# Own due times for the first four and the last five graphs of a four-layer graph network

## The chip, the cores and the metric

The kernel runs on one core of a Trainium2 chip. The metric is the device time of one execution in microseconds; before the change it is 2971.6 us, the median of three runs (2968.86 to 2973.91).

## The reference

32 graphs of 512 nodes with 256 features go through four attention layers. All graphs share one adjacency matrix and the weights, and no graph needs another's data. After each layer the result is added to the layer's input and normalised over the features.

```
x = layernorm(x + L0(x))   # 8 heads of 32: softmax(q k^T / sqrt(32), masked) v, layernorm, two matmuls with relu, layernorm
x = layernorm(x + L1(x))   # one head: e = leaky_relu(s1[n] + s2[m]), masked softmax over m, times h = x W
x = layernorm(x + L2(x))   # e = leaky_relu((x W1)(x W2)^T), masked softmax, times x W3, relu
x = layernorm(x + L3(x))   # 4 heads of 64: as layer 1, then elu
```

## The kernel before, in words

All data are float32. A graph's x is four tiles of 128 nodes by 256 features. One graph after the other is described by the same function `graph(b)`, as some 330 steps; each step is one or a few instructions of one engine, with an estimate of its time and the buffers that it reads and writes. Nothing is issued while the steps are described. A planner (`Plan.place`) then walks through the steps of all graphs and fixes the order in which each engine gets them, and each engine's queue runs in that order.

Up to five graphs are in work at once (`WAYS = 5`), so that one graph's matmuls can fill TensorE while another waits for its softmax. The planner takes, among the steps that can start earliest by its estimates, the one with the smallest due time, which `urgency(op)` gives. A step of graph b is due at b times `PACE` (90.30 us) plus a time that depends on where the step stands in the graph: the graph is planned alone once, its span is cut into ten equal parts, and the table `TENTHS` says when each part is due. In the kernel before, all graphs use `TENTHS`, and only the last two have a small offset (`LAST`). `START` holds back the load of x of the first five graphs. `STAY` makes it dearer for TensorE to change between matmuls of different array shapes.

The lines that the text below speaks of, all numbered as in the kernel before, in the order of a graph:

- L1323 loads x, L1330 stores the result (SyncE's queue). L886 transposes x or a normalised y on TensorE, L874 copies a PSUM bank out on ScalarE.
- Layer 0: L899 and L913 project to q, k and v (`wqkv`); L1016 forms scores, L1020 their exponentials (ScalarE), L1068 multiplies p by the adjacency `edge_t` (VectorE), L1075 multiplies by v. L954 adds p tiles by DMA to get the sums of the rows, which L1047 then forms on TensorE; the last graph forms them on TensorE alone (`at_once`). L967, L999 and L1002 bring the result back to nodes and divide; L1112 and L1124 are the two matmuls.
- Layer 1 and layer 3: `gates` makes factors from the scores. L1158 transposes them on TensorE, SyncE writes them to device memory (L1162) and reads them back broadcast over all partitions (L1168). Then VectorE forms p: four L1187 and one L1190 (times the adjacency) in layer 1; four L1266 and one L1273, four times, in layer 3. The products are L1197 in layer 1 and L1282 in layer 3; L1257 forms the sums of layer 3. L1309, L1311 (ScalarE) and L1314 (VectorE) are the elu.
- Layer 2: L899 and L913 again, L1220 forms scores, L1223 to L1229 the softmax, L1236 the product.
- Normalisation: L927 and L928 statistics and L934 a factor on VectorE, L937 on ScalarE. L944 are additions and products on GpSimd.

Of the kernel before, what the change touches and what calls it, by code (L numbers as in the profile page):

```python
# [28 lines left out]

WAYS = 5  # L30
PACE = 90.30
START = (0, 22.9, 53.29, 85.04, 134.37)
LAST = (-0.21, 0.21)
STAY = 4.86
TENTHS = (0, 26.21, 86.69, 92.24, 176.51, 212.02, 277.3, 313.49, 381.31, 382.21, 490.27)
@with_exitstack
def general_path(
    ctx: ExitStack,
# [31 lines left out]
    B, N, C = x.shape  # L70
# [544 lines left out]
def fast_path(  # L615
# [35 lines left out]
    B, N, C = x.shape  # L651
# [45 lines left out]
    plan = Plan({kind: len(tiles) for kind, tiles in buffers.items()})  # L697
# [621 lines left out]
    def graph(b):  # L1319

        at_once = b == B - 1
        xs = Slot("x")
        plan(SP, 450, lambda xs=xs: nc.sync.dma_start(  # L1323
            T(xs), x[b].rearrange("(c p) d -> p c d", p=P)), [], [(xs, c) for c in range(NC)],
            lag=9000)
        for layer in (layer0, layer1, layer2, layer3):
            y = layer(xs, at_once) if layer in (layer0, layer3) else layer(xs)
            xs = Slot("x")
            normalise(y, xs)
        plan(SP, 450, lambda: nc.sync.dma_start(  # L1330
            out[b].rearrange("(c p) d -> p c d", p=P), T(xs)), [xs], [], lag=8000)
# [3 lines left out]

    graph(0)
    alone = plan.place(lambda op: op.rank, 1, run=False)
    due = {}
    for t, op in plan.trace:
        tenth = min(int(10 * t / alone), 9)  # L1340
        due[op.rank] = 1e3 * (TENTHS[tenth] + (TENTHS[tenth + 1] - TENTHS[tenth]) * (10 * t / alone - tenth))
    plan.clear()
    plan.begin(-1)
    prepare()
    for b in range(B):
        plan.begin(b, 1e3 * START[b] if b < len(START) else 0.0)
        graph(b)

    def urgency(op):
        if op.graph < 0:  # L1350
            return op.rank - 1e6 if op.engine is not SP else 1e-3 * op.rank - 1e-3
        return 1e3 * (op.graph * PACE + (LAST[op.graph - B] if op.graph >= B - len(LAST) else 0.0)) + due[op.rank]
    with tc.manual_schedule(engines={mybir.EngineType.PE, mybir.EngineType.DVE,
                                     mybir.EngineType.Activation, mybir.EngineType.Pool,
                                     mybir.EngineType.SP}):
        plan.place(urgency, WAYS, 1e3 * STAY)

# [14 lines left out]
@with_exitstack  # L1372
def kernel(ctx: ExitStack, tc: tile.TileContext, *args):


    flag = ctx.enter_context(tc.tile_pool(name="flag", bufs=1))
    beyond = flag.tile([1, 1], I32, name="beyond")
    with ExitStack() as pools:
        fast_path(pools, tc, beyond, *args)
    with tc.If(tc.nc.values_load(beyond, min_val=0, max_val=1) > 0):  # L1380
        general_path(tc, *args)
# [29 lines left out]
```

## Time and profile before

| | us |
|---|---|
| median of three runs | 2971.6 |
| span of the profiled execution | 2969.2 |
| TensorE busy | 2866.9 |
| VectorE busy | 2293.7 |
| ScalarE busy | 1889.8 |
| GpSimd busy | 958.9 |

A busy share says how much of the span an engine worked; what it lacks to the whole is idle time somewhere. Where it is idle matters more than how much: with five graphs in work the middle of the kernel can be full while the beginning, where the first graphs fill up, and the end, where the last ones run out, are not.

### The profile page before, as it was taken

The page shows a single profiled execution, that of the slowest core. Times are in us where ns is not written, and L with a number is a line of the kernel's source. Part 1 is how long each engine was busy: PE and PEld are TensorE (multiplying, and loading weights), DVE is VectorE, ACT ScalarE, POOL GpSimd, SP SyncE. Part 2 cuts the span into 40 slices and gives each one's busy share as a digit, 9 for nine tenths or more (in the row PEclk, how much of TensorE's full clock was granted, in tenths as well). Part 3 has the DMA queues.
Part 4 walks back from the last instruction along what each step waited for, and adds up shares of the span by engine and source line. Part 5 has one row for each costly group of instructions (what it writes and reads, how often), then busy time and mean ns, then how long its engine had stood idle before and what let it go on. Part 6 is the DMA issues. An engine that isn't in the chain of part 4 may idle for free.

```text
span 2969.2 us, 39737 instructions
## 1 busy us (share of the span) xinstructions
PE 2866.9 (97%) x14262; PEld 1585.3 (53%) x14262; DVE 2293.7 (77%) x4076; ACT 1889.8 (64%) x4104; POOL 958.9 (32%) x898
## 2 busy tenths in 40 slices
PE   8899999999999999999999999999999999999885
PEld 3464555555555555555555555555555555555552
DVE  5567887787877878877877877888887788887775
ACT  5666576665766656766666766666766666676543
POOL 0333233332333323334332233332333333333211
PEclk9999999999999999999999999999999999999988
DMA  7536565565755566665566655566665566662232
GB/s 176 123 77 139 128 146 123 105 146 128 153 125 119 123 139 139 149 132 121 124 149 135 146 124 120 124 151 134 147 137 127 121 135 144 141 149 54 68 73 67
DMA packets 93707, 375.66 MB, mean 127 GB/s; under 512 B 8768, under 2 KB 44736, under 8 KB 57664
## 3 DMA queue, kind: packets, MB, share of 16 engines
q0 software_dynamic: 44640, 292.57, 49.0%
q1 hardware_dynamic: 48864, 80.49, 9.1%
q8 instruction: 114, 1.87, 0.2%
q14 instruction: 89, 0.73, 0.1%
HBM read 63.38 MB, written 17.10 MB: 27 GB/s over the span
## 4 chain that ended last, share of the span: by engine, by line
PE 90%; DVE 4%; DMA 3%; ACT 1%; issue 1%; POOL 0%; SPq 0%; ACTq 0%; DVEq 0%
PE bank L913 15%; PE bank L899 10%; PE bank L1016 8%; PE bank L1075 8%; PE bank L1197 8%; PE bank L1236 8%; PE bank L1282 8%; PE bank L1220 8%; PE bank L886 5%; PE bank L1112 4%; PE bank L1124 3%; PE bank L1047 2%; DMA p<-row 2%; PE bank L999 2%; PE bank L1257 1%; PE bank L967 1%
## 5 line engine op out<-in xcount | busy, mean ns | idle before, releaser
L954 POOL DMA_DIRECT2D p<-p x310 | 273.9, 886 | 1520.4 <-DMA p<-p 522.2
L1020 ACT ACTIVATE p<-bank 128x512 f32<-128x512 f32 x1024 | 546.9, 604 | 156.3 <-PE bank L1016 156.1
L1068 DVE TENSOR_TENSOR p<-p,edge_t 128x2048 f32<-128x2048 f32 x256 | 592.9, 2319 | 56.3 <-ACT p L1020 55.0
L874 ACT ACTIVATE t<-bank 128x512 f32<-128x512 f32 x640 | 369.1, 597 | 343.2 <-PE bank L1282 120.3
L944 POOL TENSOR_TENSOR y<-y,x 128x512 f32<-128x512 f32 x192 | 341.6, 1793 | 283.2 <-ACT y L1311 165.4
L927 DVE BATCH_NORM_STATS2 st<-y 128x6 f32<-128x256 f32 x768 | 314.4, 409 | 21.6 <-POOL y L944 15.3
L1075 PE MATMUL bank<-p,v 128*32 128x512 f32 x2048 | 276.8, 614 | 27.8 <-DVE p L1068 27.0
L1273 DVE TENSOR_TENSOR p<-p,edge_t 128x2048 f32<-128x2048 f32 x128 | 293.1, 2290 | 3.2
L1016 PE MATMUL bank<-t,t 32*128 32x512 f32 x2048 | 295.0, 641 | 0.0
L1266 DVE TENSOR_SCALAR p<-p,e,e 128x512 f32<-128x512 f32 x512 | 252.9, 539 | 31.6 <-DMA p<-row 31.1
L937 ACT ACTIVATE x<-y,rs,rs 128x256 f32<-128x256 f32 x512 | 269.5, 597 | 9.2 <-DVE rs L934 9.2
L1197 PE MATMUL bank<-v,p 128*128 128x257 f32 x1024 | 249.2, 390 | 19.6 <-DVE rs L934 14.8
L1236 PE MATMUL bank<-v,p 128*128 128x257 f32 x1024 | 243.6, 386 | 0.0
L1282 PE MATMUL bank<-p,v 128*64 128x512 f32 x1024 | 242.7, 614 | 0.4 <-DVE p L1273 0.4
L1220 PE MATMUL bank<-t,t 128*128 128x512 f32 x512 | 238.4, 599 | 0.0
L899 PE MATMUL bank<-t,wqkv 128*128 128x512 f32 x512 | 237.8, 597 | 0.0
L874 ACT ACTIVATE v<-bank 128x258 f32<-128x258 f32 (+2 forms) x384 | 172.2, 460 | 96.7 <-PE bank L913 94.1
L1236 PEld LDWEIGHTS bank<-v,p 128*128 128x128 f32 x1024 | 188.0, 190 | 69.6 <-ACT p L1020 21.3
L1197 PEld LDWEIGHTS bank<-v,p 128*128 128x128 f32 x1024 | 192.4, 194 | 59.1 <-issue 34.4
L1016 PEld LDWEIGHTS bank<-t,t 32*128 32x128 f32 x2048 | 82.1, 183 | 167.4 <-issue 112.8
L1241 ACT ACTIVATE y<-bank,rs 128x256 f32<-128x256 f32 x128 | 61.2, 480 | 169.8 <-DVE rs L1239 169.7
L886 PEld LDWEIGHTS bank<-ident,x 128*128 128x128 f32 x1024 | 119.1, 144 | 88.5 <-ACT x L937 36.6
(120 smaller groups left out, 4276.1 us busy)
## 6 DMA issues: line engine op xcount, KB each, us to landing
p<-p POOLq DMA_DIRECT2D x248, 1024.0 KB, 7.5
p<-row SPq DMA_DIRECT2D x32, 1024.0 KB, 6.3
p<-p POOLq DMA_DIRECT2D x62, 512.0 KB, 4.5
x<-in_x_dram SPq DMA_DIRECT2D x32, 512.0 KB, 7.0
out_dram<-x SPq DMA_DIRECT2D x32, 512.0 KB, 2.9
e<-row SPq DMA_DIRECT2D x32, 256.0 KB, 3.1
t<-in_adj_dram SPq DMA_DIRECT2D x4, 256.0 KB, 6.1
wqkv<-in_L_gnn_w_qkv_dram SPq DMA_DIRECT2D x1, 768.0 KB
```

The lines of the kernel that those rows point to most:

```text
L874: act(170 + n * 0.84, lambda: nc.scalar.activation(to(T(dst)), frm(T(src)), AF.Copy), [src], writes)
L899: nc.tensor.matmul(T(bank), T(w)[:, i, col:col + P], T(xT)[:, i, :], start=(i == 0), stop=(i == KC - 1))
L913: nc.tensor.matmul(T(bank)[:, j * width:(j + 1) * width], T(xT)[:, k, (c0 + j) * P:(c0 + j + 1) * P], T(w)[:, k, col:col + width], start=( ...
L944: pool(1500 if row is None else 1850, lambda: nc.gpsimd.tensor_tensor(T(dst)[:, w, :], T(a)[:, w, :], T(b)[:, w, :] if row is None else T( ...
L1016: nc.tensor.matmul(T(banks[j]), T(kT)[r, g, m * P:(m + 1) * P], T(qT)[r, g, :], start=True, stop=True)
L1020: act(600, lambda j=j: nc.scalar.activation(T(p)[:, j, :], T(banks[j]), AF.Exp, scale=1.0 / math.sqrt(D0)), [banks[j]], [(p, j)])
L1068: dve(2420, lambda p=p, m=m: nc.vector.tensor_tensor(T(p), T(p), T(edge_t)[:, m, :].unsqueeze(1).to_broadcast([P, J, N]), ALU.mult), [p, ( ...
L1075: nc.tensor.matmul(T(av)[j * D0:(j + 1) * D0, :], T(v)[:, m, h * D0:(h + 1) * D0], T(p)[:, j, :], start=(m == 0), stop=(m == NC - 1))
L1197: nc.tensor.matmul(T(bank)[:, :C + 1], T(p)[:, m, c * P:(c + 1) * P], T(v)[:, m, 2:C + 3], start=(m == 0), stop=(m == NC - 1))
L1220: nc.tensor.matmul(T(bank), T(xT)[:, k, m * P:(m + 1) * P], T(qT)[:, k, :], start=(k == 0), stop=(k == KC - 1))
L1236: nc.tensor.matmul(T(bank)[:, :C + 1], T(p)[:, m, c * P:(c + 1) * P], T(v)[:, m, :C + 1], start=(m == 0), stop=(m == NC - 1))
L1282: nc.tensor.matmul(T(av)[i * D3:(i + 1) * D3, :], T(q)[:, m0 + m, 2 * H3 + h * D3:2 * H3 + (h + 1) * D3], T(p)[:, 2 * m + i, :], start=(m0 ...
```

## The change

The first four graphs and the last five get tables of due times of their own, each of eleven numbers like `TENTHS`. `LAST` and its two offsets are replaced. Between the two the tables `TENTHS` and the pace stay. The tables of the last five graphs (27 to 31) let the later tenths of graphs 28 and 29 fall due very late (653.82 and 888.75 us after the graph's own start on the scale, where `TENTHS` has 490.27), and those of 30 and 31 earlier in the middle, so that the end of graph 31 comes early among its neighbours and the last three graphs are due together. `START` also changes: graphs 1 to 3 may be loaded at 0, 53.29 and 88.61 instead of 22.9, 53.29 and 85.04. It is a change of order only: every graph keeps its steps. It is meant to fill TensorE where the first graphs start and the last ones end.

```
-START = (0, 22.9, 53.29, 85.04, 134.37)
-LAST = (-0.21, 0.21)
 STAY = 4.86
+START = (0, 0, 53.29, 88.61, 134.37)
+
 TENTHS = (0, 26.21, 86.69, 92.24, 176.51, 212.02, 277.3, 313.49, 381.31, 382.21, 490.27)
+FIRST = (
+    (-14.58, 58.82, -25.93, -24.45, 99.53, 212.02, 277.3, 225.46, 380.43, 381.33, 489.39),
+    (20.46, 79.82, -4.21, 95.49, 168.52, 212.02, 277.3, 315.61, 382.59, 384.58, 492.64),
+    (10.74, 90.74, 6.57, 60.81, 176.51, 212.02, 277.3, 313.49, 383.92, 382.21, 492.29),
+    (-115.77, 26.21, 86.69, 92.58, 176.51, 210.06, 277.3, 313.49, 381.31, 382.21, 487.12),)
+LAST = (
+    (0, 25.88, 86.52, 92.24, 176.3, 211.81, 277.09, 313.28, 381.68, 376.38, 536.57),
+    (0, 27.77, 86.69, 92.22, 176.49, 212, 277.93, 316.39, 400.99, 521.01, 653.82),
+    (0, 26.21, 87.61, 91.24, 177.97, 214.48, 309.58, 343.79, 765.5, 770.4, 888.75),
+    (-0.65, 26.94, 85.87, 100.46, 141.72, 174.63, 259.04, 341.35, 397.71, 410.07, 514.93),
+    (3.71, 25.72, 94.73, 50.65, 70.79, 101.96, 247.58, 292.79, 344.82, 346.48, 489.36),)
...
-    due = {}
-    for t, op in plan.trace:
-        tenth = min(int(10 * t / alone), 9)
-        due[op.rank] = 1e3 * (TENTHS[tenth] + (TENTHS[tenth + 1] - TENTHS[tenth]) * (10 * t / alone - tenth))
+    when = {op.rank: 10 * t / alone for t, op in plan.trace}
+
+    def due(b, rank):
+        times = FIRST[b] if b < len(FIRST) else LAST[b - B] if b >= B - len(LAST) else TENTHS
+        tenth = min(int(when[rank]), 9)
+        return PACE * b + times[tenth] + (times[tenth + 1] - times[tenth]) * (when[rank] - tenth)
...
-        return 1e3 * (op.graph * PACE + (LAST[op.graph - B] if op.graph >= B - len(LAST) else 0.0)) + due[op.rank]
+        return 1e3 * due(op.graph, op.rank)
```

## The prediction

> **What bounds the kernel now.** I read the page's first part for the engine that sets the pace, then the table of stretches for where that engine is not busy, then TensorE's list of waits for the last stretch, then TensorE's timeline there.
>
> ```profile
> PE 2866.9 (97%) x14262; PEld 1585.3 (53%) x14262; DVE 2293.7 (77%) x4076; ACT 1889.8 (64%) x4104; POOL 958.9 (32%) x898
> ...
> PEclk9999999999999999999999999999999999999988
> ```
>
> TensorE is busy 97% of 2969.2 us. Only 102.3 us are idle, so no reordering can bring more than that plus what a lowered clock costs. In the table of stretches (start:end, length, then busy us of each engine, TensorE's clock, DMA share, GB/s) the idle time lies at the two ends:
>
> ```profile
> 0.00:620.00 620.00, 587.44 (x2946) 317.06 (x2947) 452.15 (x794) 387.07 (x831) 180.88 (x184) 0.99 0.60 130
> 620.00:2640.00 2020.00, 2006.10 (x10066) 1114.44 (x10064) 1608.01 (x2838) 1337.49 (x2912) 709.07 (x640) 1.00 0.62 133
> 2640.00:2970.00 330.00, 273.39 (x1257) 153.83 (x1253) 233.51 (x446) 165.22 (x362) 68.97 (x74) 0.91 0.34 79
> ```
>
> The head loses 32.6 us, the middle 13.9 us in 2020, the last 330 us lose 56.6 us, at a clock of 0.91. The waits of TensorE in that last stretch:
>
> ```profile
> PE bank L886 <- ACT x L937: 12.8, 4, 4.8
> PE bank L1257 <- DVE p L1273: 12.0, 1, 12.0
> PE bank L1197 <- DVE rs L934: 11.0, 1, 11.0
> ```
>
> These are dependences inside one graph: transposes of a layer's input waiting for its normalisation, and layers 1 and 3 waiting for the gates to come back through memory and for VectorE to build p. TensorE's timeline (start, us, then the instructions, and in brackets the idle time ahead) shows that the wait is paid twice:
>
> ```profile
> 2786.85 3.77 PE L1197 MATMUL bank<-v,p 128*128 128x257 f32 x8 [11.01 <-DVE rs L934]
> ...
> 2793.62 1.90 PE L1197 MATMUL bank<-v,p 128*128 128x257 f32 x8
> ...
> 2873.34 2.38 PE L886 MATMUL bank<-ident,x 128*128 128x128 f32 x8 [4.47 <-ACT x L937]
> 2876.40 6.35 PE L899 MATMUL bank<-t,l2m 128*128 128x512 f32 x8 [0.69 <-ACT t L874]
> ...
> 2912.69 2.38 PE L886 MATMUL bank<-ident,x 128*128 128x128 f32 x8 [4.77 <-ACT x L937]
> ...
> 2934.18 3.63 PE L1257 MATMUL bank<-p,pick 128*32 128x512 f32 x8 [11.95 <-DVE p L1273]
> ```
>
> The same eight L1197 take 3.77 us after an idle 11.01 us, and 1.90 us in the run of work.
>
> [...]while GpSimd ran three L944 from 2771.03 to 2775.04, one L1187 took 3.08 us; such instructions take 0.52 us elsewhere in VectorE's timeline.
>
> **What the change moves.** No instruction is added or removed in a graph; only urgency() differs, so each engine's queue has the same work in another order. I compared the two orders. TensorE's is identical from its 404th to its 1976th planned step (of 2391), which is from graph 4, layer 2, to graph 26, layer 1, and covers the middle. So the middle costs nothing either way: its 13.9 us of idle stay. What is left is the head (graphs 0 to 5) and the tail.
>
> Head. Graph 0's x is now loaded ahead of wqkv, and TensorE's second step becomes a projection that needs wqkv. x can come a little before the 7.63 us at which TensorE starts today, wqkv some half a microsecond later (one issue on SyncE). I take 0, between -1 and +2 us. Then the order is nearly the same up to the first transposes of graph 0's layer 1; the waits before it stay. After it, the gates' transpose of graph 0 (L1158) and the product that needs them (L1197) had about 6 us of other matmuls between them, and have 16 now (three L899 pairs of graph 4 and several steps of graph 2, by their durations in the timeline). The wait there is 3.82 us, and the L1197 behind it took 3.44 us where 1.75 is normal. That is 3.8 + 1.7 = 5.5 us gained. For graph 1 the same filler shrinks from 21 to 13 us, still above the 10 us that this round trip needs at least. (SyncE's two issues, 3.1 us landing, four L1187 and an L1190 of 2.3 us: L1158 at 2836.21 gives 2846.3 at the earliest.) Some of the gain can be lost at VectorE, so I take -4, between -7 and +2.
>
> Tail, stretch A: from graph 28's layer-3 transposes (2708.3) to graph 31's (2912.7). It lasts 204.4 us. The waits in it are 11.01 + 0.35 + 0.74 + 3.42 + 0.16 + 0.21 + 4.47 + 0.69 + 4.77 = 25.8 us; the slow instructions behind them add 1.87 + 0.87 + 1.87 + 0.55 + 1.34 + 2.65 = 9.2 us (each against the same instruction at full clock). So 169.4 us are matmuls. In the new order four layer-3 products of graph 30 (4 x 1.87), and graph 29's sums, transposes and output transposes (0.9 + 0.4 + 0.9) now stand behind graph 31's transposes: 9.7 us less, 159.7 us left. What happens to the waits:
> - Normalisation to transpose, graph 31's layer 2 (4.47 us) and layer 3 (4.77): today nothing stands between. Now three L1236 steps of graph 30 (5.5 us) and three L1282 of graph 29 (5.6 us) do. From the last matmul to the transpose takes 4.6 and 4.8 us in the timeline, so both are just covered.
> - Gates of graph 31, layer 1: 13 us of filler in place of 11. But VectorE's four L1187 and L1190 now follow each other, where before normalisations stood between them. The round trip needs 10, so 3.4 us can go.
> - Gates of graph 30, layer 1 (11.01 us): 18 us of filler in place of 11, and no run of GpSimd adds beside it.
> Is VectorE fast enough? Its work in the rest of the kernel from 2708.3 is 179.2 us. 52 of them come behind graph 31's transposes now (below), so 127 fall into stretch A, 75 to 80% of it. The middle runs at 1608/2020 = 80% with almost no wait. It fits, but with covers that are only a microsecond longer than what they hide. I allow 10 us for waits that stay or appear (between 2 and 28), most likely where TensorE's in-order queue holds a layer-3 product of graph 28 or 29 that waits for its L1273 on VectorE, with graph 31's projections behind it. Stretch A: 169.7 us, that is -34.7.
>
> Tail, stretch B: from there to the end, 56.5 us now. Here the change costs. VectorE has 29.0 us of work left today; to these come graph 30's sixteen L1266 and four L1273 (7.7 + 9.2), graph 29's output scaling, elu and normalisation (5.2) and half a normalisation of graph 28 (1.3): 52 us. Counting from graph 31's last L934 ahead of the transposes: TensorE waits for graph 30's first L1273 (3.0 us), then that product, four projections, another product: L1158 at 10.5. This is an added wait: behind that product in TensorE's queue stand graph 31's projections, and for them wait ScalarE, the gates and in the end everything. The gates are back 8.4 us later (2921.08 to 2929.52 today): 19, and VectorE has by then just worked off 20 us of the rest. Four times (4 x 0.48 + 2.29) = 16.8: 37. From the last L1273 to the end are 22.8 us today (2946.4 to 2969.2), with a hole of 5.2 us on VectorE. Into them come 10 us of graphs 29 and 30 on VectorE, half of it in the hole: 37 + 22.8 + 4.5 = 64[...]: 65. Today the same distance is 57.4 (2911.8 to 2969.2). So +8, between +3 and +20.
>
> Sum: -4 - 34.7 + 8 = -30.7 us. From the median of 2971.6 that is 2940.9.
>
> **The rivals.**
> - The waits only change place (R1). All covers are tight, and if each misses by its old amount, stretch A keeps its 25.8 + 9.2 and ends at 194.7 (-9.7); stretch B +8, head 0: 2970. [...]Against: the covers named above are longer than the holes they fill.
> - VectorE becomes the bound at the end (R2, slower). As R1, but the pile of four layer 3 (VectorE needs 52 us in stretch B[...]) stretches B by +20 and more: 2971.6 - 9.7 + 20 = 2982. For: one L1187 lost 2.5 us to L944. Against: in B only 52 of 65 us are VectorE's.
> - Everything fits (R3): waits of 2 us in A, head -7, B +3: 2971.6 - 7 - 42.7 + 3 = 2925.
> - Half (R4): waits and slow clock of 25 us in A, head -2, B +10: 2971.6 - 2 - 19.7 + 10 = 2960.
>
> **How the numbers follow.** Forecast 0.60, R3 0.13, R4 0.14, R1 0.07, R2 0.06. The forecast, R3 and R4 are faster by over 0.2% (below 2965.7): 0.87. R1 is within 0.2%, R2 slower. The range, 2921 to 2962 us, reaches from R3 to R4 and leaves R1 and R2 out with the edges of the others.
>
> **What would show it.** Right: TensorE's waits after 2640 us fall from 56.6 us idle to some 45, of which the last 17 stay; [...]TensorE's clock in the last 330 us above 0.91; graph 31's last gates (L1158) some 25 to 35 us earlier than 2921; after them VectorE near 80% busy, and three results leaving within the last 30 us. The head ends (graph 2's first L1197, 300.89 us) 2 to 6 us earlier. Wrong: a new wait of several us at an L1197 or L1236 in stretch A, L1266 or L1187 of over 2 us beside GpSimd's L944, or more than 70 us from graph 31's last transposes to the end.

## The result and the profile after

| | before | changed |
|---|---|---|
| median, us (four runs each, on the same chip) | 2970.2 | 2933.4 |
| lowest to highest, us | 2968.1 to 2973.9 | 2931.3 to 2935.2 |
| span of the profiled execution, us | 2969.2 | 2933.2 |

The ratio is 0.9874, with a 95% interval of 0.9857 to 0.9892: 37 us (32 to 42) faster. Line numbers of the changed kernel from `general_path` on are 11 higher than those of the kernel before (L1158 is L1169, L1282 is L1293), those of the experiments 4 to 8 higher (11 in the two that start from the changed kernel); the text names the role beside the line.

The first part of the page and the row of the granted clock, changed kernel:

```profile
PE 2860.7 (98%) x14262; PEld 1586.7 (54%) x14262; DVE 2290.8 (78%) x4076; ACT 1888.0 (64%) x4104; POOL 953.7 (33%) x898
...
PEclk9999999999999999999999999999999999999998
```

The instructions are the same in number. TensorE's busy time fell by only 6 us, so some 30 of the 36 us of the span were idle time. The table of stretches (columns as before) says where:

```profile
0.00:620.00 620.00, 594.46 (x2949) 320.82 (x2950) 451.09 (x794) 388.11 (x834) 175.00 (x184) 0.98 0.60 131
620.00:2640.00 2020.00, 2003.80 (x10062) 1116.01 (x10061) 1608.22 (x2839) 1337.42 (x2910) 699.70 (x640) 1.00 0.62 133
2640.00:2934.00 294.00, 262.46 (x1255) 149.85 (x1253) 231.45 (x445) 162.44 (x361) 78.96 (x74) 0.96 0.38 89
```

After 2640 us TensorE stands idle for 31.5 us in place of 56.6, and its mean clock is 0.96 in place of 0.91. The head looks fuller too, 594.5 busy us in place of 587.4; what became of that is looked at below. TensorE's waits of the last stretch, the changed kernel:

```profile
PE bank L1380 <- DVE rs L1377: 11.3, 1, 11.3
PE bank L1268 <- DVE p L1284: 7.5, 2, 7.1
PE bank L897 <- ACT x L948: 2.2, 2, 2.0
```

The first of these is the wait of the last, tiny product of the flag, behind which there is no work. The waits ahead of the layer-1 products (11.0 us before) and nearly all ahead of transposes (12.8 us) are gone. The one behind graph 31's last gates, ahead of the first sums that need them (L1257, now L1268), is down from 12.0 to 7.1.

I cut the end at the first transposes of graph 28's layer 3 and of graph 31's, in both kernels. The table of stretches, before:

```profile
2708.30:2912.70 204.40, 178.50 (x788) 105.02 (x786) 150.18 (x292) 106.81 (x238) 42.59 (x47) 0.92 0.30 72
2912.70:2970.00 57.30, 26.59 (x123) 11.33 (x123) 29.04 (x55) 16.77 (x37) 5.45 (x6) 0.74 0.13 42
```

and changed:

```profile
2709.50:2866.80 157.30, 155.25 (x736) 98.29 (x734) 126.97 (x263) 94.06 (x215) 39.26 (x40) 1.00 0.24 57
2866.80:2934.00 67.20, 37.71 (x175) 14.56 (x175) 50.38 (x91) 24.91 (x56) 15.37 (x13) 0.81 0.49 119
```

Stretch A shrank by 47.1 us and has 2 us of idle time left, at a granted clock of 1.00. Stretch B, in which VectorE's work rose from 29.0 to 50.4 us, grew by 9.9 us (56.5 to 66.4, taken to the end of each span). A starts 1.2 us later than before. 1.2 - 47.1 + 9.9 = -36.0, the difference of the spans.

### The profile page after: what moved, and what is told of

It reads as the page before. It is cut to its first block, busy times and chain, and to the rows that moved or that the text cites. A ratio compares the mean times of both kernels' runs of the same rounds, so it can differ in the third digit from the quotient of the medians.

```text
span 2933.2 us, 39746 instructions
## 1 busy us (share of the span) xinstructions
PE 2860.7 (98%) x14262; PEld 1586.7 (54%) x14262; DVE 2290.8 (78%) x4076; ACT 1888.0 (64%) x4104; POOL 953.7 (33%) x898
## 4 chain that ended last, share of the span: by engine, by line
PE 92%; DMA 3%; DVE 3%; ACT 1%; issue 1%; POOL 0%; DVEq 0%; SPq 0%; ACTq 0%
PE bank L924 15%; PE bank L910 11%; PE bank L1027 8%; PE bank L1086 8%; PE bank L1247 8%; PE bank L1293 8%; PE bank L1231 8%; PE bank L1208 8%; PE bank L897 5%; PE bank L1123 4%; PE bank L1135 3%; DMA p<-row 2%; PE bank L1058 2%; PE bank L1010 2%; DVE p L1079 1%; PE bank L978 1%
## 5 line engine op out<-in xcount | busy, mean ns | idle before, releaser
L955 POOL TENSOR_TENSOR y<-y,x 128x512 f32<-128x512 f32 x192 | 340.3, 1783 | 289.2 <-ACT y L1322 148.7
L1277 DVE TENSOR_SCALAR p<-p,e,e 128x512 f32<-128x512 f32 x512 | 256.6, 545 | 36.4 <-DMA p<-row 36.0
L1208 PE MATMUL bank<-v,p 128*128 128x257 f32 x1024 | 243.7, 385 | 3.5 <-issue 3.5
L1247 PE MATMUL bank<-v,p 128*128 128x257 f32 x1024 | 242.3, 386 | 0.0
L1293 PE MATMUL bank<-p,v 128*64 128x512 f32 x1024 | 241.7, 613 | 0.5 <-DVE p L1284 0.5
L885 ACT ACTIVATE v<-bank 128x258 f32<-128x258 f32 (+2 forms) x384 | 172.1, 460 | 95.5 <-PE bank L924 92.8
L939 DVE BATCH_NORM_AGGREGATE mv<-st 128x2 f32<-128x6 f32 x768 | 139.8, 182 | 26.3
L948 ACT ACTIVATE y<-y,rs,rs 128x256 f32<-128x256 f32 x256 | 140.0, 607 | 30.7 <-DVE rs L945 29.9
```

The source lines that it names most:

```text
L885: act(170 + n * 0.84, lambda: nc.scalar.activation(to(T(dst)), frm(T(src)), AF.Copy), [src], writes)
L948: act(600, lambda c=c: nc.scalar.activation(T(dst)[:, c, :], T(y)[:, c, :], AF.Identity, bias=T(nm)[:, c:c + 1], scale=T(rs)[:, c:c + 1]), ...
L1208: nc.tensor.matmul(T(bank)[:, :C + 1], T(p)[:, m, c * P:(c + 1) * P], T(v)[:, m, 2:C + 3], start=(m == 0), stop=(m == NC - 1))
L1247: nc.tensor.matmul(T(bank)[:, :C + 1], T(p)[:, m, c * P:(c + 1) * P], T(v)[:, m, :C + 1], start=(m == 0), stop=(m == NC - 1))
L1293: nc.tensor.matmul(T(av)[i * D3:(i + 1) * D3, :], T(q)[:, m0 + m, 2 * H3 + h * D3:2 * H3 + (h + 1) * D3], T(p)[:, 2 * m + i, :], start=(m0 ...
```

## The experiments

My theory: an early graph 30 and 31 pays because matmuls of other graphs (28, 29) stand in its waits; the head and the middle give next to nothing. The rivals: one of the two halves (late 28 and 29, or early 30 and 31) does it alone; the head shares in it; the slow clock behind a wait (in the kernel before, 0.50 over the eight products behind the wait of 11.01 us) costs nothing, since another engine sets the pace there. All ratios are against the kernel before, measured beside each kernel on the same chip, from 4 to 20 runs of each. The microseconds against before are the ratio less 1, times 2971. The last column is from one trace of each: the time from graph 26's layer-1 gates (L1158) to the end of the span. TensorE's planned order is the same in all of them from graph 4 to about there, so this column leaves out what the head and the middle did. Two traces of one kernel differ in it by 0.3 us (changed) and 1.8 (without 28). The kernel before has 554.2.

| kernel | median, us | ratio, 95% interval | us against before | graph 26's gates to the end, us |
|---|---|---|---|---|
| changed kernel, once more | 2933.0 | 0.9875 [0.9858, 0.9892] | -37 | 518.8 |
| only the last five tables | 2934.6 | 0.9880 [0.9855, 0.9904] | -36 | 520.3 |
| only head | 2968.2 | 0.9985 [0.9976, 0.9994] | -4 | 553.6 |
| only 28 and 29 | 2959.6 | 0.9964 [0.9951, 0.9977] | -11 | 543.2 |
| only 30 and 31 | 2981.3 | 1.0041 [1.0025, 1.0057] | +12 | 568.0 |
| last five without 29 | 2959.1 | 0.9957 [0.9945, 0.9970] | -13 | 541.1 |
| last five without 28, first time | 2997.0 | 1.0094 [1.0060, 1.0129] | +28 | 577.5 |
| last five without 28, again | 2991.6 | 1.0062 [1.0045, 1.0078] | +18 | 575.7 |
| the same, gates of 29 moved ahead | 2981.5 | 1.0035 [1.0024, 1.0045] | +10 | 567.3 |
| before, array kept busy in four waits | 2964.6 | 0.9981 [0.9966, 0.9996] | -6 | 548.5 |
| changed, gates of 31 first | 2937.4 | 0.9884 [0.9866, 0.9901] | -34 | 526.4 |

The rows from "only 28 and 29" to "gates of 29 moved ahead" have the head and the `START` of the kernel before. The tables are abbreviated in the edits below.

**The end alone, and the head alone.** Changed kernel with `FIRST` empty and the old `START`:

```
-FIRST = ((-14.58, ...), ...)
+FIRST = ()
-START = (0, 0, 53.29, 88.61, 134.37)
+START = (0, 22.9, 53.29, 85.04, 134.37)
```

> Only the tables of the last five graphs; START and the first four graphs as before. Theory (the gain is made in the tail, where graphs 28 to 30 stand between the dependent steps of graph 31; the head gave about 1 us): 34 to 36 us faster than before, 2934 to 2937 us, and graph 31's layer-3 gates (L1158 of before) about 42 us earlier than in the kernel before. Rival (the head gave the 4 us of the forecast): 31 to 33 us faster.

and, the other way round, the new head with the old offsets at the end (against the kernel before, the new `START` with it):

```
+FIRST = ((-14.58, ...), ...)
+LAST = (tuple(t - 0.21 for t in TENTHS), tuple(t + 0.21 for t in TENTHS))
```

> Only the tables of the first four graphs and START; the last two graphs keep their offsets of -0.21 and +0.21. Theory (the wait for the gates of graph 0 went, but an equal one came at graph 4's projections; only the earlier load of x is left): 0 to 2 us faster than before, within what can be measured. Rival (4 to 5.5 us of head, lost later in the whole kernel to something else): 4 to 6 us faster.

The end alone is 36 us faster, the changed kernel 37; the intervals overlap almost wholly. So the tail tables are the change. Graph 31's last gates leave 44 us earlier, counted from graph 26's. The head is worth -7 to -2 us on its own, by the interval of its run; the medians differ by 2.3.

**Late graphs alone, and early graphs alone.** The two halves of the tail:

```
+LAST = ((28's table), (29's table), tuple(t - 0.21 for t in TENTHS), tuple(t + 0.21 for t in TENTHS))
```

> Of the change only the tables of graphs 28 and 29 (late ends); graphs 30 and 31 have the old offsets, graph 27, START and the first graphs are as before. Theory (held-back work is filler only if graphs 30 and 31 come far enough ahead to need it, so both halves of the change are needed): 8 to 18 us faster, with waits left ahead of graph 31's layer-2 and layer-3 transposes. Rival A (the late graphs are the whole gain): 30 us or more. Rival B (they only lengthen the end): 0 or slower.

```
+LAST = ((30's table), (31's table))
```

> Of the change only the tables of graphs 30 and 31 (early middle); graphs 27 to 29 use the common table, START and the first graphs are as before. Theory (both halves needed): 12 to 24 us faster, since graph 30 now stands between graph 31's dependent steps, but graphs 28 and 29 have run out before the end. Rival A (the early last graphs are the whole gain): 30 us or more. Rival B (nothing without the late graphs): within 5 us of before.

The late half alone gives 11 us, within what was expected, with 6.3 us of waits left ahead of two transposes. The early half alone makes the kernel 12 us slower, and there the theory in its first form fell, and both its rivals too. The two halves sum to about nothing. With graph 27's table, which is in neither half, they give 36 us together; what that table does alone was not measured. TensorE's waits after 2640 us with graphs 30 and 31 alone:

```profile
PE bank L1286 <- DVE p L1277: 14.1, 6, 7.3
...
PE bank L1201 <- DVE p L1194: 10.3, 1, 10.3
PE bank L1261 <- DMA p<-p: 9.1, 2, 8.2
```

and its timeline there (start, us, instructions, and in brackets the idle time ahead):

```profile
2829.64 1.94 PE L1286 MATMUL bank<-p,v 128*64 128x512 f32 x8 [1.53 <-DVE p L1277]
2833.81 1.94 PE L1286 MATMUL bank<-p,v 128*64 128x512 f32 x8 [2.23 <-DVE p L1277]
2837.97 1.94 PE L1286 MATMUL bank<-p,v 128*64 128x512 f32 x8 [2.22 <-DVE p L1277]
2848.07 1.92 PE L1261 MATMUL bank<-p,pick 128*32 128x512 f32 x4 [8.16 <-DMA p<-p]
...
2866.68 9.07 PE L1201 MATMUL bank<-v,p 128*128 128x257 f32 x32 [10.28 <-DVE p L1194]
```

Four products of graph 29's layer 3 (L1286) follow each other in TensorE's queue, the last three 4.16 us apart, though each takes 1.94: they come at VectorE's pace for a p, which begins one at 2829.50 and the next at 2833.67 (1.91 + 2.29 us of work each). Then its sums (L1261) wait 8.16 us for the additions that DMA does. The next work of graphs 30 and 31 stands behind them in the queue. VectorE meanwhile waits for TensorE, by its list of waits from 2836 to 2870 us:

```profile
DVE e L1229 <- PE bank L971: 16.9, 1, 16.9
```

In this order the early graphs have used up the filler of that layer 3. The second form of the theory is that each layer 3 needs other graphs' matmuls spread through it, too, or the in-order queues stop there, as TensorE's did here for 8.16 us and VectorE's for 16.9.

**Which late graph is needed.** Tables of the last five, with one graph put back to `TENTHS`. Without graph 29's:

```
 (27's table), (28's table),
-(29's table),
+TENTHS,
 (30's table), (31's table)
```

> The tables of graphs 27, 28, 30 and 31; graph 29 has the common due times, and the head is that of before. In the planned order graph 29's layer 3 then stands between graph 31's layer 1 and layer 2 and is used up when graph 31's layer 3 begins. Theory (early graphs 30 and 31 pay if the work that is held back stands in their waits, from whatever graph it comes): graph 28's layer 3 and graph 29 still lie in between, so most of the 36 us stays, 18 to 34 us faster than before, and the rest is a longer end, where VectorE has only graphs 30 and 31. Rival (it is graph 29's lateness that makes it work): as with graphs 30 and 31 alone, between 5 us faster and 12 us slower, with waits of over 7 us for p or x in TensorE's list.

and without graph 28's:

```
 (27's table),
-(28's table),
+TENTHS,
 (29's table), (30's table), (31's table)
```

> The tables of graphs 27, 29, 30 and 31; graph 28 has the common due times. In the planned order its layer 3 is done before graph 31's layer 1, graph 29's layer 3 fills only the stretch around graph 31's layer 2, and the layer-3 transposes of graphs 30 and 31 stand 4 us of matmuls behind the products they need. Theory: more than half stays, but waits of 3 to 5 us come back ahead of transposes of graphs 30 and 31 (each needs 4.6 us from its last product), 12 to 28 us faster than before. Rival (only one late graph is needed, and its choice is free): 32 us or more faster, as with all tables.

The first one kept 13 of 36 us, which lies outside both expectations: more than the rival's 5, less than the theory's 18. With graph 29 used up, TensorE stands 10.8 us ahead of graph 31's last transposes, with nothing to put there:

```profile
PE bank L893 <- ACT x L944: 12.2, 4, 10.8
```

(By the tables graph 29 is due last of all, not together with the other two: its end at 29 x 90.30 + 888.75 = 3507, those of graphs 30 and 31 at 3224 and 3289. In the changed kernel the three results still leave within 5 us of each other.) The second was 28 and 18 us slower than before in its two measurements, which neither expectation had: it is also slower than graphs 30 and 31 alone (+12). VectorE's list of waits from 2800 to 2880 us, of the kernel without graph 28's table, shows where it stands:

```profile
DVE p L1273 <- DMA p<-row: 22.5, 1, 22.5
DVE ri L991 <- PE bank L974: 5.7, 1, 5.7
```

VectorE stands 22.5 us ahead of graph 29's first p, which waits for gates that come back through memory. It runs nothing else from 2832.11 to 2854.65, and what graphs 30 and 31 need of it next stands behind in the planned order. I read this as the cause; the next run moves those gates.

**Graph 29's gates moved ahead.** The kernel without graph 28's table, and in it the transpose of graph 29's layer-3 gates on TensorE planned ahead of the last of graph 31's layer-2 transposes and of its projections and scores, in place of behind them:

```
+    return 1e3 * (due(op.graph, op.rank) - (70 if op.graph == B - 3 and 253 <= op.rank <= 272 else 0.0))
```

> The kernel of the run without graph 28's table, with one single instruction moved: the transpose of graph 29's layer-3 gates on TensorE stands ahead of graph 31's layer-2 transposes, projections and scores in place of behind them. VectorE's order is the same, instruction by instruction. In that run VectorE stood 22.5 us ahead of graph 29's first p, with everything of graphs 30 and 31 queued behind it. Theory (VectorE's in-order queue, held by a layer 3 whose gates come late, is what makes early graphs slower than before): the gates' transpose comes some 13 us earlier, VectorE's wait falls to about 10 us, and the time falls by 8 to 13 us, to 2984 to 2989. Rival (the loss comes from elsewhere, the layer-3 products at VectorE's pace or the slow clock): within 3 us of 2997.

> The kernel without graph 28's table once more, to stand beside the one with the moved gates on the same chip: 2997 us, between 2990 and 3004.

It is not quite the single instruction of the expectation: four projections of graph 29 come four transposes earlier with it, some copies on ScalarE and one memset on GpSimd change places too. VectorE's and SyncE's orders are the same, instruction by instruction.

The kernel is 10.1 us faster than the run beside it (2981.5 against 2991.6), within the 8 to 13 expected; from graph 26's gates to the end it is 8.4. VectorE's list of waits, 2815 to 2862 us:

```profile
DVE p L1273 <- DMA p<-row: 10.2, 1, 10.2
```

The wait fell by 12.6 us (22.8 in the run beside it), and the transposes' start from 2847.23 to 2836.97. With VectorE's order unchanged, this shows that the wait of VectorE's queue for those gates is on the path, and is worth 8 to 10 of the 18 us. Of the 10.2 us that remain, 7.4 are the way from that transpose through memory (2836.97 to 2844.37). Where the other 8 to 10 us go (TensorE's 11.1 us ahead of layer-3 products, the 11.0 us of sums waiting for DMA) was not taken apart.

**The price of the slow clock.** The kernel before with transposes of the identity, whose result nobody reads, ahead of four of its waits:

```
+KEEP = {(30, 177): 90, (31, 177): 26, (31, 195): 34, (31, 253): 36}
...
+    for _ in range(KEEP.get((op.graph, op.rank), 0)):
+        self.busy(op.slots[-1])
```

> The kernel before, with transposes of the identity (0.11 us each) put into TensorE's queue ahead of four waits of the last two graphs: 90 ahead of graph 30's first layer-1 product, 26 ahead of graph 31's, 34 ahead of its layer-2 and 36 ahead of its layer-3 transposes. The waits stay as long as they are, only the array works through most of them. Theory (the slower matmuls behind these waits, 9.2 us in sum, are on the path that sets the end): 5 to 9 us faster, the eight matmuls of the layer-1 product behind the first wait take about 1.9 in place of 3.77 us, and the clock in the last 330 us is above 0.91. Rival (VectorE, ScalarE or the gates set the pace behind a wait, so the slow matmuls cost nothing): within 2 us of before. If the 90 are too many and outlast the wait, up to 3 us of the gain are lost.

The waits stay, the array works through most of them: at the first it is idle for 1.22 us in place of 11.01. The mean granted clock after 2640 us is 0.96 in place of 0.91. TensorE's timeline at the first of them:

```profile
2774.62 9.99 PE L702 MATMUL bank<-ident 128*128 128x128 f32 x90
2785.83 1.97 PE L1202 MATMUL bank<-v,p 128*128 128x257 f32 x8 [1.22 <-DVE rs L939]
```

The eight matmuls behind take 1.97 us, where they took 3.77 in the kernel before, at a granted clock of 0.50 (2786.85 to 2790.62 us); the eight at 2793.62 us of that trace took 1.90 at 1.00. The kernel is 6 us faster, with an interval from 1 to 10; the medians differ by 6.8, and from graph 26's gates to the end the trace is 5.8 us shorter. So the slow matmuls were on the path. How many of the 9.2 us counted for them it brought back, the interval is too wide to say.

**What limits the end now.** The changed kernel, and in it graph 31 from its layer 2 to the gates of its layer 3 due 30 us earlier:

```
+    return 1e3 * (due(op.graph, op.rank) - (30 if op.graph == B - 1 and 195 <= op.rank <= 272 else 0.0))
```

> The changed kernel, with one more edit: the due times of graph 31 from its layer 2 up to the gates of its layer 3 are 30 us earlier. In the planned order its last transposes, projections and gates then stand ahead of graph 30's first layer-3 product, which waits for p, and graph 31's last normalisation stands ahead of graph 30's first p on VectorE. Theory (the end is the pile of layer 3 on VectorE, and the gates' way through memory is partly open in it: VectorE stands about 5 us between graph 30's last p and graph 31's first): the last gates 4 to 6 us earlier, VectorE's hole goes, the end 2 to 5 us earlier, 2928 to 2932. Rival 1 (VectorE's work alone sets the end): within 1.5 us of the changed kernel. Rival 2 (the earlier transposes meet their normalisation unfilled, and the hole only moves to TensorE ahead of them): 2 us slower or more.

> The changed kernel once more, to set the others beside it on one chip: 2933 us, between 2930 and 2937.

By the medians it is 4.5 us slower than the changed kernel beside it, with intervals that overlap: no gain, where the theory had 2 to 5 us. TensorE's waits there:

```profile
PE bank L1380 <- DVE rs L1378: 14.7, 1, 14.7
PE bank L1293 <- DVE p L1284: 5.1, 2, 4.4
PE bank L1268 <- DMA p<-p: 4.4, 2, 2.2
```

The second rival has the nearest number, but not the mechanism: there is no wait ahead of graph 31's transposes. Counted from graph 26's gates, graph 31's last gates left 7.7 us earlier than in the run beside it, but graph 30's left 7.9 later. VectorE then waits 2.7 us for graph 30's gates; it starts its pile of layer 3, the p of graphs 30 and 31, 6.0 us later and ends it 0.9 earlier. Behind the pile come 35.7 us to the end, in place of 27.1: a hole of 4.6 us opens ahead of a reciprocal (L995), and VectorE has 17.7 us of work left there in place of 14.6. So the edit traded one graph's gates for another's. It shows that the last gates alone don't set the end; whether VectorE's work does (it is busy 50.4 of the 66.4 us of stretch B) is not shown. No version of these runs beats the changed kernel.

## Why the prediction was right

- **Bound and place.** TensorE's idle time at the end was named as what can be won. It fell by 25.1 us there, to 31.5 us, where I had expected some 45; the end alone brings 36 of the 37 us. The middle was put at nothing, because its order is the same. In the two traces the layer-1 gates of graphs 26 to 28 do come within 1 us of where they came before (graph 28: 2590.68, now 2590.03). That does not show that nothing happened in between, as the next point says.
- **Head, -4 us.** One trace of each kernel is not enough here, since kernels with the same head differ by up to 6 us at graph 4. Nine traces of these experiments have the old head and `START`, four the new ones. When the layer-1 gates of a graph leave TensorE, in us:

| graph | nine with the old head, mean | four with the new head, mean |
|---|---|---|
| 4 | 454.7 to 460.5, 457.7 | 452.2 to 454.0, 453.3 |
| 12 | 1178.3 to 1186.2, 1182.0 | 1175.5 to 1179.1, 1177.8 |
| 13 | 1266.1 to 1274.1, 1269.9 | 1268.6 to 1272.2, 1270.9 |
| 26 | 2410.4 to 2416.6, 2413.8 | 2411.1 to 2414.8, 2413.4 |

  At graph 4 the new head is 4.4 us ahead, as forecast, and it stays so up to graph 12. From graph 12 to 13 all four lose it: this stretch takes them 92.8 to 93.4 us, and 87.9 in all nine others. VectorE stands there 5.0 to 5.5 us for layer-3 gates on their way back through memory, and then TensorE 3.3 to 3.8 us for a p of layer 0. VectorE's timeline there and TensorE's, of the changed kernel:

```profile
1236.01 1.00 DVE L1277 TENSOR_SCALAR p<-p,e,e 128x512 f32<-128x512 f32 x2 [5.02 <-DMA p<-row]
...
1243.03 1.93 PE L1086 MATMUL bank<-p,v 128*32 128x512 f32 x8 [3.28 <-DVE p L1079]
```

  So the middle, put at nothing, was not neutral, and why those gates come late is open. At graph 26 the means are 0.4 us apart, less than the traces scatter; the runs with the head alone leave a gain of 2 to 7.

  How the 4.4 us come about was foreseen only in part. The wait of 3.8 us for graph 0's gates is gone, but one nearly as long came in its place. TensorE's timeline of the changed kernel at 147 us:

```profile
147.21 7.11 PE L910 MATMUL bank<-t,wqkv 128*128 128x512 f32 x12 [2.63 <-ACT t L885]
```

  Twelve projections of graph 4 that were to be filler now wait for ScalarE themselves, 2.6 us, and run 7.11 us at a granted clock of 0.76, where twelve such took 5.40 at 1.00, at 13.70 us of the same trace. Part of the gain comes from the start, which I had put at nothing: TensorE begins at 5.1 to 5.3 us in the four, at 7.5 to 8.4 in the nine. The rest was not traced.
- **Stretch A, -34.7 us; measured -47.1.** The mechanism held: the gates of graph 31's layer 3 leave at 2877.73 in place of 2921.08, 43 us earlier, where 25 to 35 were forecast. The term that was mis-sized is the 10 us allowed for waits that stay or appear; they are 2. The covers that I called a microsecond longer than what they hide were enough in every case but one. TensorE's timeline where graph 31's layer-1 products follow, ahead of which 3.4 us were lost before, and at the one wait that is left, ahead of graph 31's last transposes:

```profile
2816.04 7.10 PE L1208 MATMUL bank<-v,p 128*128 128x257 f32 x32
2822.97 5.36 PE L1247 MATMUL bank<-v,p 128*128 128x257 f32 x24
...
2866.77 0.33 PE L897 MATMUL bank<-ident,x 128*128 128x128 f32 x1 [2.01 <-ACT x L948]
```

  The rest of the difference is work that moved out of A: 169.4 - 155.1 = 14.3 us of matmuls, where I had counted 9.7. TensorE's work in B rose by 11.1 us; the 3.2 us between the two are not accounted for.
- **Stretch B, +8 us; measured +9.9.** VectorE's 52 us came out as 50.4. The added wait of 3.0 us for graph 30's first p came out as 0.2, yet graph 31's gates left 11.9 us after its last normalisation factor (2865.86 to 2877.73), in place of 10.5; the first of the two products ahead of them took 2.86 us, the second 1.94. Gates back in 8.4 us: 9.85 (2877.73 to 2887.58). Four p in 16.8 us: 18.5 (2887.58 to 2906.07), one group of rows taking longer beside GpSimd, as in VectorE's timeline of the changed kernel:

```profile
2887.58 1.91 DVE L1277 TENSOR_SCALAR p<-p,e,e 128x512 f32<-128x512 f32 x4 [1.95 <-DMA p<-row]
...
2896.22 3.37 DVE L1277 TENSOR_SCALAR p<-p,e,e 128x512 f32<-128x512 f32 x3
```

  Three of L1277 took 3.37 us, four elsewhere 1.91; GpSimd ran two additions (L955), 4.28 us together, from 2894.57. Three took 1.46 us in the run with the gates of 31 first, so these took 1.9 us more. The forecast of 65 us had 1 us for this, my estimate. That GpSimd is what held them up is read from the overlap alone.
- **The slow clock as part of the waits** (9.2 us counted in A). Keeping the array busy in the kernel before gained 6 us (1 to 10) while the waits stayed, which fits them and does not fix their size.
- **The rivals.** R1 (the waits change place) did not come about with all tables. It is what happens with part of them: with graphs 30 and 31 alone, and without graph 28's. R2 (VectorE's pile) had stretch B at +20 and more; it came out at +10, and how much of that is the pile is not shown. R4 (half) expected 25 us of waits and slow clock in A, over ten times what is left. R3 (2925), which had 2 us of waits in A, was right there and too good in head and B.

The forecast of 2940.9 us was 7.5 too high. By the spans, stretch A came out 12.4 us better than forecast and stretch B 1.9 worse; the 4 us of the head, by the means of the traces won at graph 4 and lost again by graph 13, did not show at the start of A, which came 1.2 later. That is -5.3 us, so the miss in A and the loss in the middle partly cancelled; the other 2.2 are the median of before (2970.2 beside the changed kernel, 2971.6 in the forecast) and the difference between spans and medians.

## What to carry to other kernels

Where several independent chains run out together, order their ends by what each wait needs as filler, and count the filler for VectorE's queue as well as for TensorE's: a late chain that stands at the head of an in-order queue stops all chains behind it, as VectorE's 22.5 us without graph 28's table show. The parts of such an edit don't add up: here late graphs 28 and 29 brought 11 us, early 30 and 31 cost 12, and all five tables brought 36. A wait can cost more than its own time: here the eight matmuls behind 11.01 us of it took 3.77 us, at a granted clock of 0.50, and 1.90 at 1.00. Compare the same matmuls behind a wait and in a run of work to see how much. And a steady stretch with an unchanged order can still take another time (here 92.8 to 93.4 us in place of 87.9): compare several traces before a gain or loss of a few us is put down to an edit.

## What the runs showed of the hardware

- In the steady middle, whose planned order is the same in all these kernels, a stretch that takes 87.9 us can take 5 to 7 us more: 92.8 to 93.4 us from the gates of graph 12 to those of 13 in all four traces with the new head, 94.5 and 94.8 from graph 18 to 19 in two of the nine with the old one. In each of these six VectorE stands 5.0 to 6.0 us ahead of a layer-3 p for gates on their way through memory. Why they come late is not shown.
- With graphs 30 and 31 alone, products of layer 3 that follow each other on TensorE without other work come every 4.16 us, at VectorE's pace for a p (4.17 us from one to the next, 1.91 + 2.29 us of work), though one takes 1.94 us.
